# A graph network's edge sums on one core: the copies of the tiles' products out of PSUM move from ScalarE to VectorE, and ScalarE brings in a tile of rows in every ninth half chunk

## The chip, the core and the metric

The kernel runs on one core of a Trainium2 chip. The core has TensorE (PE: matrix products, with PEld for its weight loads), VectorE (DVE), ScalarE (ACT), GpSimd (POOL) and SyncE (SP), each with its own queue of instructions that it takes in order; engines wait for one another through semaphores. Transfers are started by three of these queues: SyncE and ScalarE start plain ones, GpSimd the indirect ones that gather rows by a list of numbers.

The metric is the device's time in microseconds (us) for one execution. Before the change it is 23621.08 us, the median of three runs (23593.12 to 23628.34).

## What is computed

There are 50000 nodes with 128 features each, 800000 edges between them (every pair in both directions) and one loop per node, 850000 rows of (src, dst, relation) sorted by dst. Two layers of a relational graph network run one after the other, then a residual and a layer norm:

```python
def _rgcn_layer(h, src, dst, rel, basis, w_comp, loop_w, bias):
    W = jnp.einsum('rb,bio->rio', w_comp, basis)
    seg = dst.astype(jnp.int32) * N_REL + rel.astype(jnp.int32)
    agg = jax.ops.segment_sum(h[src], seg, num_segments=N_ENT * N_REL)
    agg = agg.reshape(N_ENT, N_REL, -1)
    msg = jnp.einsum('nri,rio->no', agg, W)
    out = msg + h @ loop_w + bias
    return jax.nn.relu(out)
...
x = _layernorm(x + _L0_gnn_ref(x, ...), axis=-1)
```

All is in float32; there are 16 relations and 8 bases.

## The kernel before

The edges without the loops are cut into 6250 tiles of 128 edges. Ten tiles (K) make a chunk, five (PER) a half chunk: 625 chunks (C) and 1250 half chunks in each of the two layers. For each tile the kernel

- brings in the 128 source rows, 512 bytes each, into a buffer named g;
- multiplies them on TensorE (L1136) with a one-hot table that carries the edges' weights in each basis and their place among the chunk's nodes. The tile's product is 96 columns wide; the five products of a half chunk stand side by side in one PSUM tile, pa, of which there are three;
- copies pa into aT (L1150), where four chunks (BATCH) are gathered.

When four chunks are complete, TensorE multiplies aT with the bases (L815), the result by_slot is copied (L819), turned (L824), spread over four columns of nodes by VectorE (L798), and added to the nodes' sums (L859). Beside this run the loops' part (L745 to L780: transposes, products with the bases on TensorE, products and sums on VectorE), the weights and one-hot tables of the chunks to come (L638, L667, L950, on VectorE), and the ending of each group of 512 nodes (L881 to L894). In the first layer VectorE also sorts the edge lists as they are needed.

The rows come in by three ways. GpSimd gathers a whole tile with one indirect transfer (L186) into a ring of 30 buffers (RING x PER); it is given the gathers of the half chunk that lies 30 tiles ahead, and each waits until its buffer's product is done. The other two ways are row by row: SyncE and ScalarE bring in some tiles with 128 single transfers (L1046), and load the rows' addresses, 32 at a time, into registers (L1039). Which tiles they take is set by `takers`: the last tile of some half chunks, one in 9 for SyncE and one in 10 for ScalarE, by `SPANS = (9, 10)`. The first such half chunk is number max(SPANS) + LEAD + 6, which is 24 for SyncE. Each of the two has three buffers (HELD) for this.

The order is written out by hand (`manual_schedule`): every queue has its instructions in the order in which the loops below emit them. After each tile's product, `beside` emits one step of everything else: the rows of the tiles that SyncE and ScalarE are bringing in (`copying`; a tile's 128 rows are spread over the 45 or 50 tile steps that end 8 half chunks, LEAD, before its use), the loops' part (`owning`), the batch's sums (`summing`), the weights (`weighing`) and the ending groups. So the rows stand in ScalarE's queue between its copies, and in SyncE's between its other loads and stores.

Of the kernel before, what the change touches and what calls it, by code (L numbers as in the profile page):

```python
# [54 lines left out]
K = P // WN  # L55
# [13 lines left out]
WEIGHTS = AT * PER * 8  # L69
BITS_AT_ONCE = BANK - WEIGHTS  # L70
RING = 6
SPANS = (9, 10)
LEAD = 8
THEN = 3
HELD = 3
SEMS = 8
LOADED = 32
# [15 lines left out]
def tile_rgcn_resnorm(  # L93
# [15 lines left out]
    nc = tc.nc  # L109
    N, D = x.shape  # L110
    NR, NB = w_comp1.shape
    E = edges.shape[1] // 3
    R, M = -(-E // RUN), E - N
    C = -(-M // (K * P))
# [83 lines left out]
    def column(j, first, ap):  # L198
# [10 lines left out]
    apart = [  # L209
        [consts.tile([P, D], F32, name=f"g{RING * PER + HELD * i + j}") for j in range(HELD)] for i in range(len(APART))  # L210
    ]
    came = [[tc.alloc_semaphore(f"came{i}_{j}") for j in range(SEMS)] for i in range(len(APART))]
    uses = [0] * len(APART)
    earliest = (max(SPANS) + LEAD + 1) // 2 + 1
    far = consts.tile([P, len(ROWS), P], I32, name="far")

    def takers():

        of, first = {}, max(SPANS) + LEAD + 6
        for i, span in enumerate(SPANS):  # L220
            for q in range(first + span * i // len(SPANS), 2 * C - LEAD, span):
                while q in of:
# [388 lines left out]
    def chunked():  # L611
        with (
# [182 lines left out]
            def spread_out(c, to, of):  # L795

                k, pair = ks(c) * WN, of.shape[1]
                nc.vector.tensor_tensor(  # L798
                    to[:k],
                    of[:k, :, None, :].to_broadcast([k, pair, J, D]),  # L800
                    which[:k, c : c + pair, :, None].to_broadcast([k, pair, J, D]),
                    op=OP.mult,
                )
                return to

            def pair_of_slots():
                return sb.tile([P, 2, J, D], F32, name="slots", bufs=BATCH // 2)

            def slots_of_batch(c, aT, st, n):

                for _ in range(2):
                    yield
                ps = ps_o.tile([P, BANK], F32, name="po")
                for b in range(NB):
                    nc.tensor.matmul(  # L815
                        ps[:, : BATCH * S], BASIS[n][:, b, :], aT[:, b, :], start=b == 0, stop=b == NB - 1
                    )
                by_slot = sb.tile([P, BATCH * S], F32, name="by_slot", bufs=1)
                nc.scalar.copy(by_slot, ps[:, : BATCH * S])  # L819
                for _ in range(NB - 2):  # L820
                    yield
                po = ps_o.tile([P, BANK], F32, name="po")
                for q in range(BATCH):
                    nc.tensor.transpose(po[:S, q * P : (q + 1) * P], by_slot[:, q * S : (q + 1) * S], ident)  # L824
                    if q == 1:
                        yield
                for q in range(0, BATCH, 2):
                    pair = spread_out(c + q, pair_of_slots(), po[:, q * P : (q + 2) * P].rearrange("s (q d) -> s q d", q=2))
                    st[c + q], st[c + q + 1] = pair[:, 0], pair[:, 1]
                    yield  # L830
# [45 lines left out]
            def finish(g, n):  # L876
# [5 lines left out]
                if n == 0:  # L882
                    yield
                    nc.scalar.activation(ls, ls, AF.Relu)
                    for _ in range(THEN):
                        yield
                    nc.sync.dma_start(of_group(H1, g), ls)
                else:
                    nc.vector.scalar_tensor_tensor(ls, total, 0.0, xws.pop(g)[:m], op0=OP.max, op1=OP.add)
                    yield  # L890
                    yield from normed(ls, J, m, ls, sb)
                    for _ in range(THEN):
                        yield
# [3 lines left out]
            def done(steps):  # L897
                for _ in steps:
                    pass
# [38 lines left out]
            for n, of in enumerate((x, H1)):  # L938
# [19 lines left out]
                def sum_up(c):  # L958
                    at = c % BATCH * S
                    for st[c] in slots(c, ks(c), aTs[c // BATCH][:, :, at : at + S], n):  # L960
                        yield
# [53 lines left out]
                tiles = -(-M // P)  # L1015
# [5 lines left out]
                def row_by_row(i):  # L1021
# [3 lines left out]
                    mine = sorted(q for q in taken_by if taken_by[q] == i)  # L1025
                    for q, before in zip(mine, [mine[0] - SPANS[i], *mine]):
                        while now[1] < before - LEAD:
# [3 lines left out]
                        uses[i] += 1  # L1031
                        to, sem, group = apart[i][use % HELD], came[i][use % SEMS], f"rows{i}_{use}"
                        j = max(j for j in range(len(ROWS)) if ROWS[j] <= q)
# [46 lines left out]
                def fetch(some):  # L1080

                    for t in some:
                        if t < tiles:
                            if t % WIDE == WIDE // 2:
                                numbers(t // WIDE + 1)
                            if not alone(t):
# [4 lines left out]
                                held[t] = rows[k], came_of[k], 16 * filled_times[k], group  # L1091
                                read_now.append(group)

                numbered, held = {}, {}
                numbers(0)
                now, made = [0, 0], [0]
                owning = own_of_all()
                copying = [row_by_row(i) for i in range(len(APART))]
                for c in range(C):
                    now[0] = c  # L1100
                    if n == 0 and c:

                        next(coming, None)
                        while ready[0] + 1 < len(ROWS) and 2 * min(C, c + FETCH + earliest) > ROWS[ready[0] + 1]:
                            next(coming)
                    if c == 0:
                        fetch(range(RING * PER))
                        nc.vector.tensor_copy(table, COMP[n].rearrange("p r b -> p b r"))
                        weighing = weights(0)
                        done(weighing)  # L1110
                        hots[0] = hot_of(0)
                        hots[1] = hot_of(1)
                        if n == 0:
                            for _ in range(LBITS + 3):
                                next(first_runs)
                    if c % 2 == 0 and c + 2 < C:
                        weighing = weights(c + 2)
                    hot = hots.pop(c)
                    if c % BATCH == 0:
                        aTs[c // BATCH] = hp.tile([P, NB, BATCH * S], F32, name="aT")  # L1120
                    aT, place_of = aTs[c // BATCH], c % BATCH * S
                    if c > ALONE:
                        done(summing)
                        summing = sum_up(c - 1)
                    elif c % BATCH == 0:
                        summing = slots_of_batch(c - BATCH, aTs[c // BATCH - 1], st, n) if c else iter(())
                    for k in range(0, K, PER):
                        m = min(PER, ks(c) - k)
                        if m > 0:
                            pa = ps_a.tile([P, BANK], F32, name="pa")  # L1130
                        for i in range(PER):
                            now[1] = 2 * c + k // PER
                            if i < m:
                                t = c * K + k + i
                                row, sem, count, group = held.pop(t)
                                product = nc.tensor.matmul(  # L1136
                                    pa[:, i * NB * WN : (i + 1) * NB * WN],
                                    row,
                                    hot[:, k + i].rearrange("e b w -> e (b w)"),
                                    start=True,  # L1140
                                    stop=True,
                                ).wait_op(sem, count, "sem-ge")
                                tc.declare_fence(product.ins, group=group)
                                tc.declare_no_dep(product.ins, group=group, reason="it waits for their semaphore itself")
                            if i == m - 1:
                                at = c * K + k + RING * PER
                                fetch(range(at, at + PER))
                                if n == 0 and c == 0 and k == 0:
                                    done(first_runs)
                                nc.scalar.copy(  # L1150
                                    aT[:, :, place_of + k * WN : place_of + (k + m) * WN].rearrange(
                                        "d b (i w) -> d i b w", w=WN
                                    ),
                                    pa[:, : m * NB * WN].rearrange("d (i b w) -> d i b w", i=m, w=WN),
                                )
                            beside(k + i, c, owning, summing, weighing)
                    if c + 2 < C:
                        hots[c + 2] = hot_of(c + 2)
                    for one in added_in(c + 1) if c + 1 < C else ():
                        masks[one] = masks_of(one)  # L1160
                    if n == 0 and c == 3:
                        beginning.close()
                    if n == 0 and c == C - 1:
                        done(coming)
                        count_up(pr)
# [199 lines left out]
```

## Time and profile before

| what | value |
| --- | --- |
| device time, median of 3 runs | 23621.08 us |
| device time of the profiled execution | 23644.94 us |
| its span, first to last instruction | 23642.9 us |
| busy: PE, PEld | 11528.9 us (49%), 7370.5 us (31%) |
| busy: DVE, ACT, POOL | 10300.2 us (44%), 2154.3 us (9%), 11393.7 us (48%) |
| mean granted TensorE clock | 0.699 |
| DMA | 1014.02 MB in 585877 packets, mean 43 GB/s |

No engine is busy for half of the span, and instructions that only start a transfer are not counted as busy. In 40 equal slices of the span the engines' shares hardly change, so the kernel has one long steady stage:

```
PE   4544445445554444444555444544444444444445
DVE  5444444444444444344444444444444444444444
ACT  0000000000000000000000000000000000000001
POOL 5444444444444444444454444444444444444444
```

A digit is the busy share of a slice in tenths. A row of a group names line, engine, operation, the tile written and the tiles read, shapes and count; then busy time and the mean ns of one; then the idle time of the engine just before such instructions and what ended most of it. An engine with a q behind its name (SPq, ACTq, POOLq) is its queue starting transfers. "issue" and "remote" are idle times that the profile can put down to no other engine.

### The profile page before, as it was taken

The numbers are of one execution on the slowest core, as the hardware profiler recorded it, in microseconds if no ns is written. First come the engines' busy times: TensorE is split into PE (matmuls) and PEld (weight loads), VectorE is DVE, ScalarE is ACT, GpSimd is POOL, SyncE is SP. The second block draws the span as 40 slices with busy tenths as digits, with TensorE's granted clock in tenths as the row PEclk, the third lists the DMA queues.
The fourth block names the chain that finished last, engine by engine and source line by source line (L and its number), as shares of the span: only waits on it lengthen the run. The fifth ranks groups of instructions, "written<-read, shape, count | busy, mean of one in ns | idle before, by whom it ended". The sixth has DMA issues, their size and how long they took to land. (4 is left out here: it accounts for less than half of the span.)

```text
span 23642.9 us, 256085 instructions
## 1 busy us (share of the span) xinstructions
PE 11528.9 (49%) x43954; PEld 7370.5 (31%) x43954; DVE 10300.2 (44%) x11737; ACT 2154.3 (9%) x4309; POOL 11393.7 (48%) x12017
## 2 busy tenths in 40 slices
PE   4544445445554444444555444544444444444445
PEld 3333333333333333233333233332333233332333
DVE  5444444444444444344444444444444444444444
ACT  0000000000000000000000000000000000000001
POOL 5444444444444444444454444444444444444444
PEclk7677676766676767766766667667766677766667
DMA  2111111111111111111111111111111111111111
GB/s 58 49 46 43 45 45 47 47 42 46 48 44 41 40 39 40 40 40 40 37 48 43 42 41 41 42 42 41 41 42 42 41 42 42 41 43 41 42 42 40
DMA packets 585877, 1014.02 MB, mean 43 GB/s; under 512 B 267619, under 2 KB 336739, under 8 KB 577970
## 3 DMA queue, kind: packets, MB, share of 16 engines
q0 software_dynamic: 385360, 793.04, 12.9%
q1 hardware_dynamic: 133308, 186.60, 2.5%
q10 hardware_dynamic: 65552, 17.90, 0.3%
q14 instruction: 1302, 10.67, 0.1%
q8 instruction: 355, 5.82, 0.1%
HBM read 924.87 MB, written 71.59 MB: 42 GB/s over the span
## 5 line engine op out<-in xcount | busy, mean ns | idle before, releaser
L186 POOL DMA_INDIRECT g<-H,at x5992 | 5674.1, 947 | 6132.7 <-PE pa L1136 3704.1
L186 POOL DMA_INDIRECT g<-in_x_dram,at x5992 | 5695.0, 950 | 6012.9 <-PE pa L1136 3600.5
L1136 PE MATMUL pa<-hot,g 128*128 128x96 f32 x25000 | 4340.2, 318 | 6655.2 <-DMA g<-H 2811.6
L1136 PEld LDWEIGHTS pa<-hot,g 128*128 128x128 f32 x25000 | 4236.9, 236 | 8680.6 <-issue 3305.7
L772 DVE TENSOR_TENSOR by<-po,lw 128x512 f32<-128x512 f32 x1568 | 1076.8, 687 | 8061.4 <-PE po L765 5019.4
L859 PE MATMUL pn<-slots,own 120*128 120x512 f32 x4128 | 2763.6, 796 | 1915.6 <-issue 968.9
L765 PE MATMUL po<-basis,hT 128*128 128x512 f32 x3136 | 2134.6, 769 | 2054.3 <-issue 875.6
L815 PE MATMUL po<-aT,basis 128*128 128x480 f32 x4960 | 2451.9, 655 | 1000.3 <-ACT aT L1150 615.2
L1150 ACT COPY aT<-pa 128x480 f32<-128x480 f32 x2500 | 1394.3, 558 | 14372.9 <-issue 7359.7
L780 DVE TENSOR_REDUCE ls<-by 128x128 f32<-128x1152 f32 (+1 forms) x784 | 1656.4, 2113 | 583.9 <-DMA out_dram<-ls 427.8
L667 DVE TENSOR_REDUCE fixed<-terms 128x80 f32<-128x1280 f32 x1250 | 1864.8, 1492 | 30.4
L638 DVE TENSOR_TENSOR terms<-kinds,fixed 128x1280 f32<-128x1280 uint8 x1250 | 1849.6, 1480 | 12.1
L815 PEld LDWEIGHTS po<-aT,basis 128*128 128x128 f32 x4960 | 1079.6, 224 | 2183.3 <-issue 1544.2
L859 PEld LDWEIGHTS pn<-slots,own 120*128 120x128 f32 x4128 | 899.7, 247 | 2601.8 <-issue 1615.9
L950 DVE TENSOR_TENSOR hot<-fixed,own 128x960 f32<-128x960 f32 x1250 | 1439.3, 1152 | 313.4 <-PE pa L1136 255.7
L765 PEld LDWEIGHTS po<-basis,hT 128*128 128x128 f32 x3136 | 597.2, 237 | 2112.6 <-issue 943.2
L798 DVE TENSOR_TENSOR slots<-po,which 120x1024 f32<-120x1024 f32 (+1 forms) x630 | 761.6, 1209 | 971.2 <-remote 511.2
L881 DVE TENSOR_TENSOR pn<-pn,ls 128x512 f32<-128x512 f32 x98 | 68.1, 695 | 930.9 <-PE pn L859 394.8
L1073 ACT CAST at<-src 128x20 int32<-128x20 uint16 x626 | 129.5, 207 | 3701.2 <-issue 3688.1
L838 DVE TENSOR_SCALAR own<-col,node 120x256 f32<-120x256 f32 (+1 forms) x1250 | 426.0, 341 | 9.8 <-PE pn L859 8.6
L881 DVE TENSOR_TENSOR ls<-pn,ls 128x512 f32<-128x512 f32 x98 | 67.2, 685 | 752.3 <-PE pn L859 328.4
L703 DVE TENSOR_TENSOR both_kinds<-col,po 128x256 uint8<-128x256 f32 (+1 forms) x50 | 20.8, 416 | 841.8 <-PE po L695 476.2
(143 smaller groups left out, 4155.4 us busy)
## 6 DMA issues: line engine op xcount, KB each, us to landing
g<-in_x_dram SPq DMA_DIRECT2D x17408, 0.5 KB
g<-H SPq DMA_DIRECT2D x17408, 0.5 KB
g<-in_x_dram ACTq DMA_DIRECT2D x15616, 0.5 KB
g<-H ACTq DMA_DIRECT2D x15616, 0.5 KB
g<-in_x_dram,at POOLq DMA_INDIRECT x5992
g<-H,at POOLq DMA_INDIRECT x5992
H<-ls SPq DMA_DIRECT2D x97, 256.0 KB
xw<-in_x_dram SPq DMA_DIRECT2D x97, 256.0 KB
```

The source lines that it names most:

```text
L186: return nc.gpsimd.indirect_dma_start(out=to, out_offset=None, in_=of, in_offset=bass.IndirectOffsetOnAxis(ap=idx, axis=0))
L638: nc.vector.tensor_tensor(terms, kinds[:, :, None, :].to_broadcast([P, k, NB, NR]), table[:, None, :, :].to_broadcast([P, k, NB, NR]), op= ...
L667: nc.vector.tensor_reduce(to[:, : ks(i)], terms, AX.X, OP.add)
L765: nc.tensor.matmul(hb[:m], hT[:, j, :m], BASIS[n][:, b : b + few, :].rearrange("p b d -> p (b d)"), start=True, stop=True,)
L772: nc.vector.tensor_tensor(by[:m, b : b + few, :], hb[:m].rearrange("p (b d) -> p b d", d=D), lw[:m, j, g % T, b : b + few, None].to_broadc ...
L780: nc.vector.tensor_reduce(ls[:m, j, :], by[:m].rearrange("p b d -> p d b"), AX.X, OP.add)
L798: nc.vector.tensor_tensor(to[:k], of[:k, :, None, :].to_broadcast([k, pair, J, D]), which[:k, c : c + pair, :, None].to_broadcast([k, pair ...
L815: nc.tensor.matmul(ps[:, : BATCH * S], BASIS[n][:, b, :], aT[:, b, :], start=b == 0, stop=b == NB - 1)
L859: nc.tensor.matmul(sums[g], own, of[:k].rearrange("s j d -> s (j d)"), start=c == first(g), stop=c == final(g),)
L950: nc.vector.tensor_tensor(hot[:, : ks(c)], pm[:, : ks(c), :, None].to_broadcast([P, ks(c), NB, WN]), own[:, : ks(c), None, :].to_broadcast ...
L1136: product = nc.tensor.matmul(pa[:, i * NB * WN : (i + 1) * NB * WN], row, hot[:, k + i].rearrange("e b w -> e (b w)"), start=True, stop=Tr ...
L1150: nc.scalar.copy(aT[:, :, place_of + k * WN : place_of + (k + m) * WN].rearrange("d b (i w) -> d i b w", w=WN), pa[:, : m * NB * WN].rearr ...
```

## The change

The copy of a half chunk's products from pa to aT is no longer emitted right behind the half chunk's last product. It is kept (`to_take`) and emitted behind the first product of the next half chunk, one tile later. VectorE makes it in chunks 8 to 616; before and after these ScalarE still does. The by_slot copy stays on ScalarE and is emitted one step of the batch's sums later, and one step fewer lies between it and the transposes that read it. `SPANS` becomes (9, 9): ScalarE brings in a tile in every ninth half chunk. With it the first half chunk with such a tile becomes 23.

```diff
-SPANS = (9, 10)
+SPANS = (9, 9)
 LEAD = 8
 THEN = 3
+COPIED = 8
...
+                yield
                 by_slot = sb.tile([P, BATCH * S], F32, name="by_slot", bufs=1)
                 nc.scalar.copy(by_slot, ps[:, : BATCH * S])
-                for _ in range(NB - 2):
+                for _ in range(NB - 3):
                     yield
...
+                to_take = []
+
+                def taken_out():
+
+                    by_vector = COPIED <= now[0] < C - COPIED
+                    (nc.vector.tensor_copy if by_vector else nc.scalar.copy)(*to_take)
...
+                            if i == 0 and c + k:
+                                taken_out()
                             if i == m - 1:
                                 at = c * K + k + RING * PER
                                 fetch(range(at, at + PER))
                                 if n == 0 and c == 0 and k == 0:
                                     done(first_runs)
-                                nc.scalar.copy(
+                                to_take[:] = [
                                     aT[:, :, place_of + k * WN : place_of + (k + m) * WN].rearrange(
                                         "d b (i w) -> d i b w", w=WN
                                     ),
                                     pa[:, : m * NB * WN].rearrange("d (i b w) -> d i b w", i=m, w=WN),
-                                )
+                                ]
+                                if c * K + k + m == tiles:
+                                    taken_out()
```

In the whole program ScalarE's single rows go from 31232 to 34560 (26 tiles more), SyncE's stay 34816, and GpSimd's gathers fall by 26. The first place to look at is ScalarE's queue around the by_slot copy of one batch in the second layer. Before:

```order
L1150 COPY aT<-pa 128x5x8x12
L1046 DMA g_122<-H_57 1x512 x2
L1039 TENSOR_LOAD far
L1046 DMA g_120<-H_57 1x512 x5
L819 COPY by_slot<-po 128x480
L1046 DMA g_120<-H_57 1x512 x5
L1150 COPY aT<-pa 128x5x8x12
L1046 DMA g_120<-H_57 1x512 x2
L751 COPY hT<-po 128x4x128
```

And now, around the same copy (lines have moved by one or two):

```order
L1075 CAST at<-src 128x20
L1048 DMA g_122<-H_57 1x512 x17
L752 COPY hT<-po 128x4x128
L821 COPY by_slot<-po 128x480
L1048 DMA g_122<-H_57 1x512 x8
L602 ACTIVATE sd<-mv,eps 128x4
L1048 DMA g_122<-H_57 1x512 x2
L1041 TENSOR_LOAD far
L1048 DMA g_122<-H_57 1x512 x18
```

The aT copies between the rows are gone, so ScalarE's queue has only the hT and by_slot copies and the ending of a group between rows that wait for other engines, and by_slot now stands behind hT.

The second place is VectorE's queue in the second layer, where a group of nodes ends and a batch is spread into slots. Before:

```order
L638 TENSOR_TENSOR terms<-kinds,fixed 128x1280
L667 TENSOR_REDUCE fixed<-terms 128x80
L881 TENSOR_TENSOR pn<-pn,ls 128x512
L889 SCALAR_TENSOR_TENSOR ls<-pn,xw 128x512
L950 TENSOR_TENSOR hot<-fixed,own 128x960
L838 TENSOR_SCALAR own<-col_128,node_126 120x128
L598 BN_STATS st<-ls 128x6
```

Now:

```order
L1101 COPY aT<-pa 128x5x8x12
L639 TENSOR_TENSOR terms<-kinds,fixed 128x1280
L668 TENSOR_REDUCE fixed<-terms 128x80
L883 TENSOR_TENSOR pn<-pn,ls 128x512
L891 SCALAR_TENSOR_TENSOR ls<-pn,xw 128x512
L952 TENSOR_TENSOR hot<-fixed,own 128x960
L840 TENSOR_SCALAR own<-col_128,node_126 120x128
L1101 COPY aT<-pa 128x5x8x12
L599 BN_STATS st<-ls 128x6
```

The rest of VectorE's queue keeps its order; a copy stands in it twice in each chunk, ahead of the weights of a chunk to come and behind its one-hot table and its masks.

## The prediction, made before the changed kernel had run

> **What bounds the kernel now.** The reading starts with the view of who waited for whom, to see whether any compute engine is short. These are its rows on TensorE's products, on GpSimd's gathers and on ScalarE's copies: total us, times, longest.
>
> ```profile
> POOL g L186 <- PE pa L1136: 7304.7, 784, 37.3
> ...
> ACT aT L1150 <- PE pa L1136: 5011.9, 682, 35.2
> ...
> PE pa L1136 <- DMA g<-H: 2811.6, 123, 38.5
> ...
> PE pa L1136 <- DMA g<-in_x_dram: 2398.1, 105, 39.5
> ...
> PE pa L1136 <- ACT aT L1150: 683.6, 118, 38.1
> ...
> PE po L815 <- ACT aT L1150: 615.2, 83, 14.8
> ```
>
> GpSimd waits 7304.7 us for a free row buffer, so it is not short. TensorE waits 2811.6 + 2398.1 = 5209.7 us for gathered rows, but in only 228 waits of about 23 us. That is close to the number of tiles that SyncE brings in row by row, and far from the number of GpSimd's gathers. So the second look is the view of tile g, which has every transfer of rows: count, shortest/median/longest ns, first and last start.
>
> ```profile
> L1136 PE MATMUL pa<-hot,g x25000: 242/275/529, 41.5 to 23626.6; 128*128 128x96 f32 x199
> ...
> L1046 SPq DMA_DIRECT2D g<-in_x_dram x17408: 1/228/1486, 104.4 to 11758.0; - x198
> ...
> L1046 SPq DMA_DIRECT2D g<-H x17408: 1/228/1532, 11830.8 to 23562.6; - x198
> ...
> L1046 ACTq DMA_DIRECT2D g<-in_x_dram x15616: 2/235/1407, 166.5 to 11688.8; - x198
> ...
> L1046 ACTq DMA_DIRECT2D g<-H x15616: 2/235/1462, 11939.6 to 23494.0; - x198
> L186 POOL DMA_INDIRECT g<-in_x_dram,at x5992: 939/947/1816, 30.3 to 11801.7; - x200
> L186 POOL DMA_INDIRECT g<-H,at x5992: 939/947/1122, 11830.1 to 23609.1; - x200
> ```
>
> SyncE issues 17408 rows in each layer, 128 to a tile: 136 tiles, one in every 9 half chunks. Its two streams last 11653.6 and 11731.8 us. Together that is 23385.4 of the span's 23642.9 us; only 257.5 us lie before, between and after them. Does the stream ever rest? The view of SyncE's own waits has as its longest row:
>
> ```profile
> SPq L887 <- ACT ls L884: 62.4, 3, 42.2
> ```
>
> So it hardly waits. And TensorE starts again when a tile of it is complete, as the transfers issued up to 6062.5 us (first fence) and TensorE's row of the timeline (second) show:
>
> ```profile
> g<-in_x_dram SPq DMA_DIRECT2D x8832, 0.5 KB
> ```
>
> ```profile
> 6063.74 0.53 PE L1136 MATMUL pa<-hot,g 128*128 128x96 f32 x1 [20.80 <-DMA g<-in_x_dram]
> ```
>
> 8832 is 69 times 128: the 69th tile's last row had been issued by 6062.5 us, and TensorE's wait of 20.80 us ended at 6063.74. **SyncE's issuing of rows is the bound.** Everything else has 5209.7 / 272 = 19.2 us of cover for each SyncE tile.
>
> **What sets SyncE's pace.** A median row takes 228 ns to issue, yet the mean is 23385.4 / 34816 = 0.672 us. Five windows of 15 us, by engine (busy us and instructions of PE, PEld, DVE, ACT, POOL; then TensorE's clock, DMA share, GB/s), tell why:
>
> ```profile
> 14907.00:14922.00 15.00, 0.00 (x0) 0.00 (x0) 0.00 (x0) 0.00 (x0) 0.00 (x0) 0.50 0.03 11
> 2458.00:2473.00 15.00, 8.12 (x15) 4.19 (x16) 14.47 (x17) 2.25 (x5) 0.00 (x0) 0.56 0.06 21
> 11831.00:11846.00 15.00, 6.88 (x22) 5.22 (x22) 12.40 (x10) 0.56 (x1) 11.34 (x13) 0.50 0.26 76
> 11849.00:11864.00 15.00, 9.55 (x30) 7.43 (x30) 0.00 (x0) 0.56 (x1) 11.34 (x13) 0.50 0.20 53
> 12976.00:12991.00 15.00, 10.16 (x36) 5.49 (x36) 10.04 (x9) 0.56 (x1) 10.64 (x12) 1.00 0.21 54
> ```
>
> The transfers issued in the same five windows, one fence for each:
>
> ```profile
> g<-H SPq DMA_DIRECT2D x39, 0.5 KB
> ```
>
> ```profile
> g<-in_x_dram SPq DMA_DIRECT2D x40, 0.5 KB
> g<-in_x_dram ACTq DMA_DIRECT2D x38, 0.5 KB
> ```
>
> ```profile
> g<-H SPq DMA_DIRECT2D x24, 0.5 KB
> g<-H,at POOLq DMA_INDIRECT x13
> ```
>
> ```profile
> g<-H,at POOLq DMA_INDIRECT x13
> g<-H SPq DMA_DIRECT2D x7, 0.5 KB
> ```
>
> ```profile
> g<-H,at POOLq DMA_INDIRECT x12
> g<-H ACTq DMA_DIRECT2D x12, 0.5 KB
> g<-H SPq DMA_DIRECT2D x8, 0.5 KB
> ```
>
> Without gathers SyncE issues 39 or 40 rows in 15 us, 0.385 us each with its loads of offsets, and 38 rows of ScalarE beside them, or a VectorE that is busy for 14.47 us, take nothing from it. With gathers back to back it issues 24 rows while the run is young, and 7 or 8 later, the same with ScalarE silent (7) as with 12 of its rows (8). So a gather costs SyncE (15 - 24 x 0.385) / 13 = 0.44 us early in a run and (15 - 7 x 0.385) / 13 = 0.95 us late. On the mean: 23385.4 - 34816 x 0.385 = 9981 us over 11984 gathers, 0.83 us each.
>
> The Trainium skill reads such a stall otherwise: its page "DMA: Bandwidth & Descriptors", in the section "Issuing engines are not separate DMA queues", says that transfers from all issuing engines end on the same 16 DMA engines and interleave, and that several issuers save only the sequencers' time. By that a tile moved from GpSimd to ScalarE would relieve SyncE of nothing, and the first term below would be 0, the sum +12.6 us. The windows speak against it: SyncE falls from 39 rows to 7 while the DMA engines are busy to a share of only 0.20.
>
> **The change part by part.** The sum is made against the profiled execution, 23644.94 us by the device's time, 0.10% above the median of the three runs, 23621.08.
>
> *ScalarE's tiles in every 9th half chunk.* Its spacing falls from 10 to 9, so it brings 135 tiles a layer in place of 122, 26 more in all, and GpSimd gathers 26 fewer. For SyncE this is worth between nothing and a gather's whole slot in a back-to-back run, 15 / 12 = 1.25 us (last window); I take the mean of 0.83: **-21.6 us**. The 26 tiles are 3328 more rows on ScalarE's queue. Their price to SyncE lies between 0 and, if the two queues excluded each other, 0.235 us a row, 782 us. The two pairs of windows (40 against 39, 8 against 7) stand at 0: **0 us**.
>
> *SyncE's tiles one half chunk earlier.* They stand at 23 + 9k instead of 24 + 9k, again 136 a layer. The stream starts where it did, and one more half chunk follows its end. In the second layer the last SyncE row is issued at 23562.6 and the last product starts at 23626.6: 10 half chunks in 64 us, 6.3 us each (from 0, if the tail is shortened elsewhere, to 9.5, the span over 2500 half chunks). Twice that: **+12.6 us**.
>
> *The copies.* 2436 of 2500 copies go from ScalarE to VectorE. Two rows of groups, with mean ns after the busy time:
>
> ```profile
> L772 DVE TENSOR_TENSOR by<-po,lw 128x512 f32<-128x512 f32 x1552 | 1066.1, 687 | 8001.7 <-PE po L765 4962.2 <-remote 1216.5 <-issue 1186.2
> ...
> L1150 ACT COPY aT<-pa 128x480 f32<-128x480 f32 x2500 | 1394.3, 558 | 14372.9 <-issue 7359.7 <-PE pa L1136 5011.9 <-remote 1541.1
> ```
>
> VectorE reads 512 elements from PSUM in 687 ns, so a copy of 480 should take 480/512 of it, 0.64 us (an estimate, between ScalarE's 0.558 and the 0.687 itself): 1559 us, or 5.7 us per SyncE tile. Queued behind the waiting copy are VectorE's weights, one-hot tables and loop products, for which TensorE waits. Even if all 5.7 us land on TensorE's path, and none of the 683.6 + 615.2 us (4.8 per tile) in which TensorE waited for ScalarE's copies comes back, the cover of 19.2 us holds: **0 us**. Without that cover it would be +1559 us.
>
> *The by_slot copy one step later.* It stays on ScalarE, its readers stand where they stood: **0 us**, under the same cover.
>
> Sum: -21.6 + 12.6 = **-9 us**. Against the median that is 23612 us: no change. A measurement of this kernel tells about 0.2%, 47 us, from no change.
>
> **The rivals.** *A: ScalarE becomes the bound (slower).* In the second layer its rows took (23494.0 - 11939.6) / 15616 = 0.740 us, 94.7 us a tile; SyncE's period, which it now has to keep, is 23385.4 / 272 = 86.0. It must win back 8.7 us a tile. It can: before its copies ScalarE's datapath sat idle for 5011.9 us until a product was done, and 1541.1 us with no releaser told, up to 26.9 us for each of its 244 tiles, though rows were issued in part of that. The rival decides if less than 8.7 us come back. Each us that is missing costs 272 us; with 3 missing the time is 24.43 ms, with nothing won 25.98 ms. Against it: TensorE's waits for rows, 228, are fewer than SyncE's tiles alone, and a ScalarE that lags no longer waits. Chance 0.10.
>
> *B: gathers run in longer runs (slightly slower).* TensorE, no longer held at ScalarE's copies, frees row buffers more evenly, and GpSimd's 784 waits become fewer. A gather moved from early to late in a run costs 0.95 - 0.44 = 0.51 us, and one such per SyncE tile 272 x 0.51 = 139 us. B decides from a third of a gather per tile; with one, 23751 us. Chance 0.14.
>
> *C: the runs get shorter (faster).* The same price with the other sign: VectorE, in order and fuller, holds TensorE at more places, GpSimd pauses more often, and ScalarE, free of its waits, uses the pauses for its rows. One gather per tile from late to early gives 23473 us, one and a half 23404. For it: 5.7 us of new VectorE work per tile against 4.8 us of waits that go. Chance 0.27. The skill's page "SBUF — State Buffer", section "Who interferes with whom", would add to C: a VectorE copy in a two-port mode locks GpSimd out for its whole length. But "VectorE: DVE Perf Modes", section "Why PSUM operands drop a tier", takes a source in PSUM out of that mode, so I add nothing for it; no row here shows such a copy.
>
> *D: ScalarE's rows do cost SyncE.* At up to 0.235 us for each of 3328 rows: 24.39 ms. The windows with ScalarE's rows speak against it. Chance 0.05.
>
> **How the numbers follow.** The forecast, within 0.2% either way (23565 to 23659), has 0.44. Faster is C, 0.27; slower are A, B and D, 0.29. The range takes in B and C to one and a half gathers per tile, 23612 less or plus 209: 23400 to 23830; outside are A, D and the ends of B and C, about 0.2. The predicted time is the forecast's, 23612.
>
> **What would show it.** Right: SyncE's two streams again fill all but some 270 us of the span; GpSimd has 11958 gathers; TensorE still waits some 5000 us for gathered rows, in about 230 long waits; its waits for ScalarE's aT copies are gone. A: waits for rows that end when ScalarE's tiles are complete, and more than 272 of them. B or C: the number of GpSimd's waits for TensorE's products clearly under or over 784, and SyncE's mean row off 0.672 us. D: SyncE's rows slower in windows without gathers. The forecast is wrong above all if SyncE's streams no longer fill the span.

## The result, and the profile after

On the chip of the prediction the changed kernel takes 23524.13 us, the median of six runs (23493.53 to 23546.47); the kernel before takes 23608.2 us (six runs, three of them those of before the prediction). The ratio is 0.9965, with an interval of 0.9954 to 0.9975: 84 us faster. The time lies in the predicted range, 88 us under the forecast of 23612. It is no "no change" by the bound of 0.2% that the prediction set itself: it falls on rival C's side, and it is the width that the range gave to C, not the sum of -9 us, that takes it in.

That is half of the result. The experiments below ran on chips 12, 7 and 15, and there **the kernel before takes 15118.9 to 15139.3 us, and the same changed kernel is 4.2% slower** (timed on chip 7). The first measurements name no chip. That theirs was another one is taken from the times alone; it is called the first chip here. So there are two questions: where 84 us went on the first chip, and why the sign turns on the others.

First the page of the changed kernel on the first chip: its span, its busy times and the chain that ended last, which could be followed back through a part of the span only.

```profile
span 23544.3 us, 262043 instructions
...
PE 11586.5 (49%) x43954; PEld 7419.2 (32%) x43954; DVE 11688.0 (50%) x14173; ACT 838.5 (4%) x1873; POOL 11364.1 (48%) x11991
...
SPq 12%; issue 7%; PE 1%; ACTq 0%; DVE 0%; DMA 0%; ACT 0%; another core or an unknown queue 0%; DVEq 0%
```

The copies have moved: ScalarE is busy for 838.5 us in place of 2154.3, VectorE for 11688.0 in place of 10300.2. Then the view of tile g, with the transfers of rows: count, shortest/median/longest ns, first and last start.

```profile
L1048 SPq DMA_DIRECT2D g<-in_x_dram x17408: 1/228/1477, 103.9 to 11666.0; - x198
...
L1048 SPq DMA_DIRECT2D g<-H x17408: 1/228/1450, 11745.0 to 23461.1; - x198
...
L1048 ACTq DMA_DIRECT2D g<-in_x_dram x17280: 2/228/1450, 145.3 to 11532.5; - x199
...
L1048 ACTq DMA_DIRECT2D g<-H x17280: 2/228/1412, 11852.9 to 23346.5; - x199
L187 POOL DMA_INDIRECT g<-in_x_dram,at x5979: 939/947/1819, 30.2 to 11714.9; - x200
L187 POOL DMA_INDIRECT g<-H,at x5979: 939/947/1083, 11744.4 to 23510.7; - x200
```

SyncE's streams last 11562.1 us (11653.6 before) and 11716.1 us (11731.8 before). Together they lose 107.2 us; the stretch between them grows by 6.2 us, the tail by 2.9 us, and the start loses 0.5 us: 98.6 us between the two profiled spans. Most of the gain, 91.5 us, is in the first layer. And who waited for whom, in the rows that answer to those shown before:

```profile
POOL g L187 <- PE pa L1145: 7059.8, 728, 48.6
...
PE pa L1145 <- DMA g<-H: 2934.2, 121, 41.5
...
PE pa L1145 <- DMA g<-in_x_dram: 2288.7, 94, 38.6
...
PE po L766 <- ACT hT L752: 924.0, 66, 29.4
...
PE po L816 <- DVE aT L1101: 752.6, 87, 46.4
...
PE pa L1145 <- DVE aT L1101: 97.8, 10, 39.0
```

TensorE's waits for rows are 5222.9 us in 215, against 5209.7 us in 228. Its waits for copies have moved: the tiles' products wait for aT for 97.8 us in place of 683.6, while the products with the bases wait 752.6 us in place of 615.2 for aT and 924.0 in place of 858.9 for hT. The bound is still SyncE's rows.

### The profile page after: what moved, and what is told of

The parts are those of the page before. It is cut to its first block, busy times and chain, and to the rows that moved or that the text cites. A ratio compares the mean times of both kernels' runs of the same rounds, so it can differ in the third digit from the quotient of the medians.

```text
span 23544.3 us, 262043 instructions
## 1 busy us (share of the span) xinstructions
PE 11586.5 (49%) x43954; PEld 7419.2 (32%) x43954; DVE 11688.0 (50%) x14173; ACT 838.5 (4%) x1873; POOL 11364.1 (48%) x11991
## 5 line engine op out<-in xcount | busy, mean ns | idle before, releaser
L1145 PE MATMUL pa<-hot,g 128*128 128x96 f32 x25000 | 4289.6, 317 | 5679.3 <-DMA g<-H 2934.2
L816 PE MATMUL po<-aT,basis 128*128 128x480 f32 x4960 | 2572.1, 681 | 1366.1 <-DVE aT L1101 752.6
L766 PE MATMUL po<-basis,hT 128*128 128x512 f32 x3136 | 2118.3, 764 | 1753.8 <-ACT hT L752 924.0
L1101 DVE COPY aT<-pa 128x480 f32<-128x480 f32 x2436 | 1567.6, 648 | 2672.5 <-PE pa L1145 2143.6
L826 PE MATMUL po<-ident,by_slot 128*120 128x128 f32 x1240 | 311.5, 343 | 743.5 <-DVE by L773 423.0
L826 PEld LDWEIGHTS po<-ident,by_slot 128*120 128x120 f32 x1240 | 190.9, 188 | 764.1 <-issue 634.0
L746 PE MATMUL po<-ident,h_own 32*128 32x32 f32 x3136 | 328.2, 249 | 60.1 <-issue 54.1
```

The costliest lines, as they stand in the source:

```text
L766: nc.tensor.matmul(hb[:m], hT[:, j, :m], BASIS[n][:, b : b + few, :].rearrange("p b d -> p (b d)"), start=True, stop=True,)
L816: nc.tensor.matmul(ps[:, : BATCH * S], BASIS[n][:, b, :], aT[:, b, :], start=b == 0, stop=b == NB - 1)
L1101: (nc.vector.tensor_copy if by_vector else nc.scalar.copy)(*to_take)
L1145: product = nc.tensor.matmul(pa[:, i * NB * WN : (i + 1) * NB * WN], row, hot[:, k + i].rearrange("e b w -> e (b w)"), start=True, stop=Tr ...
```

## The experiments

All times below are against the kernel before on the same chip. "The copies alone" and "SPANS alone" undo one half of the change each; the third keeps the new order but leaves the copies on ScalarE; the fourth gives SyncE, not ScalarE, the wider spacing. In the second the diff is against the kernel before, in the others against the changed kernel.

```diff
e1_copies_only
-SPANS = (9, 9)
+SPANS = (9, 10)
e2_spans_only
-SPANS = (9, 10)
+SPANS = (9, 9)
e3_late_on_scalar
-SPANS = (9, 9)
+SPANS = (9, 10)
-COPIED = 8
+COPIED = 400
e4_sync_every_10th
-SPANS = (9, 9)
+SPANS = (10, 9)
```

> The changed kernel with ScalarE's tiles back in every 10th half chunk; the copies on VectorE, the later place and the later by_slot copy stay. GpSimd has 11984 gathers again and SyncE its old places. If the gain of 84 us came from 26 fewer gathers and their 0.83 us alone, the time is that of before, about 23600 us. If it came from the copies (gathers in shorter runs, ScalarE's queue without waits for products), about 85 - 9 us of it is here: some 23530 us, and SyncE's first stream stays some 80 us shorter than before.

> The kernel before with only the spacing changed to (9, 9); the copies stay on ScalarE. By the forecast's terms (26 gathers fewer, a longer tail) -9 us: about 23600 us. If ScalarE cannot bring in a tile in 86 us while its queue waits at copies (rival A), each us that it is short costs 272 us: 23.8 ms and more, with waits of TensorE that end when ScalarE's tiles are complete.

> Spacing (9, 10) and all copies on ScalarE, but emitted one tile later, and the by_slot copy one step later, as in the changed kernel. If the later places matter, some of the 84 us are here; if VectorE's taking the copies matters, the time is that of before, 23600 us within 30.

> The changed kernel with SyncE's tiles in every 10th half chunk, ScalarE's in every 9th: 122 SyncE tiles a layer instead of 136, some 28 more gathers. If SyncE's issuing is the bound at 0.385 us a row and 0.83 to 0.95 us a gather, a period of 10 half chunks takes 89 to 91 us: 22.05 to 22.45 ms, 5 to 6% faster. If its stream only fills the span because its rows are spread over it and something else sets the pace, the time stays at 23.5 ms.

Measured on chip 12, where the kernel before takes 15138.93 us:

| run | time, us | ratio | interval |
| --- | --- | --- | --- |
| e1, copies alone | 15197.70 | 1.0039 | 1.0025 to 1.0053 |
| e2, SPANS alone | 15757.12 | 1.0407 | 1.0393 to 1.0421 |
| e3, late, on ScalarE | 15141.86 | 1.0002 | 0.9992 to 1.0011 |
| e4, SyncE every 10th | 15306.25 | 1.0110 | 1.0092 to 1.0128 |

None of the expectations was made for a chip of 15.14 ms, so the numbers in them miss. What bounds the kernel here is seen in e3, which takes as long as the kernel before. The groups of its page (busy, mean ns, idle before) and the waits' row:

```profile
L187 POOL DMA_INDIRECT g<-in_x_dram,at x5992 | 5695.6, 951 | 1845.5 <-issue 1701.3
L187 POOL DMA_INDIRECT g<-H,at x5992 | 5671.8, 947 | 1849.7 <-issue 1720.5
```

```profile
POOL g L187 <- issue: 3421.9, 11138, 19.6
```

A gather takes 0.95 us as on the first chip, and GpSimd hardly waits for anybody: it goes from one gather to the next after a pause of 3421.9 / 11138 = 0.31 us that no engine ends. 5695.6 + 5671.8 + 3421.9 = 14789 of the span's 15140.0 us are this. **GpSimd is the bound here**, and SyncE keeps up with it. Why it can is in one row of e3's tile g against the same row of the changed kernel on the first chip, the MOVE that stands before each row's transfer:

```profile
L1048 SPq MOVE g<-in_x_dram x17408: 29/29/38, 86.5 to 7498.4; - x198
```

```profile
L1048 SPq MOVE g<-in_x_dram x17408: 1/29/1409, 103.9 to 11666.0; - x198
```

An instruction of 29 ns that moves no data takes up to 1409 ns in this row on the first chip and never over 38 here. No stall such as the prediction put at 0.83 us a gather is seen here.

But e2, with 26 gathers fewer, is 4% slower. Two theories: the fuller row queue of ScalarE is the bound (A'), or the place of the copies behind rows (Q). The changed kernel itself belongs beside e2, and spacings on both sides of it. The diffs are against the changed kernel; e5 has none.

```diff
e6_scalar_every_18th
-SPANS = (9, 9)
+SPANS = (9, 18)
e7_both_every_12th
-SPANS = (9, 9)
+SPANS = (12, 12)
e8_both_every_8th
-SPANS = (9, 9)
+SPANS = (8, 8)
```

> The changed kernel as it is, beside the kernel before on the chip of these runs. Where the kernel before takes about 23.6 ms (SyncE's issuing of rows is the bound): 0.9965 of it again, about 23525 us. Where it takes about 15.14 ms (GpSimd is the bound, a gather's slot is 15 / 12 = 1.25 us or 0.947 us and the pause behind it): theory G, that only the gathers and the copies' place count, gives the time with the copies alone moved, 15197.7 us, less 26 x 1.25 = 32 us, 15165 us, ratio 1.002. Rival Q, that ScalarE's fuller row queue holds TensorE whoever makes the copies (its hT and by_slot copies stand behind rows too), gives the 15757 us of the run in which only SPANS was changed, or a good part of it: over 15300 us.

> The changed kernel with SPANS = (9, 18): ScalarE brings in 67 tiles a layer in place of 135 (and SyncE 135 in place of 136), so GpSimd gathers 138 more in all. Where SyncE's issuing is the bound: 138 x 0.83 = +115 us from the changed kernel, about 23.62 ms, and over 23.9 ms slower is excluded; if ScalarE's rows did cost SyncE (rival D, up to 0.235 us each of 17408 fewer), up to 4 ms faster. Where GpSimd is the bound: 138 x 1.25 = +172 us from the changed kernel, about 15.34 ms; if ScalarE's queue holds TensorE (rival Q), the same or faster than the changed kernel.

> The changed kernel with SPANS = (12, 12): 102 + 101 tiles a layer row by row in place of 136 + 135, GpSimd gathers 136 more in all (12094). Where SyncE's issuing is the bound, its two streams become 26112 x 0.385 + 12094 x (0.83 to 0.95) = 20.1 to 21.5 ms and the time 20.3 to 21.8 ms, over 7% faster; if the streams are only the place where TensorE waits, and something that doesn't scale with SyncE's rows is the bound, 23.5 to 23.7 ms. Where GpSimd is the bound: 136 x 1.25 = +170 us, about 15.34 ms.

> The changed kernel with SPANS = (8, 8): 153 + 152 tiles a layer row by row, GpSimd gathers 68 fewer in all (11890). Where SyncE's issuing is the bound, its streams become 39168 x 0.385 + 11890 x 0.83 = 24.95 ms and the time 25.2 ms, 7% slower. Where GpSimd is the bound: 68 x 1.25 = -85 us from the changed kernel, about 15.08 ms, faster than both kernels, unless ScalarE's or SyncE's rows become the bound there: at 0.24 to 0.40 us a row (31 to 51 us a tile, a period of 48) that is near.

Measured on chip 7, where the kernel before takes 15118.89 us:

| run | time, us | ratio | interval |
| --- | --- | --- | --- |
| e5, the change as it is | 15757.20 | 1.0421 | 1.0407 to 1.0436 |
| e6, ScalarE every 18th | 15236.97 | 1.0079 | 1.0063 to 1.0094 |
| e7, both every 12th | 15236.36 | 1.0077 | 1.0059 to 1.0096 |
| e8, both every 8th | 17299.39 | 1.1442 | 1.1421 to 1.1463 |

The change takes 15757.20 us, e2 15757.12: who makes the copies is worth nothing once SPANS is (9, 9). That compares two chips whose kernels before differ by 20 us; e11 below makes the same comparison on chip 12. Theory G, 15165 us, is wrong by 592 us, and the number of theory Q came out. Fewer rows on ScalarE (e6) bring the time down by 520 us although GpSimd has 138 gathers more, and e8 goes up to 17.3 ms, where its expectation had 15.08 ms for a kernel bound by GpSimd and called ScalarE's rows near to being the bound. The expectations of e6 and e7, 15.34 ms, are 100 us too high. e6 has 112 gathers more than the kernel before and takes 118 us more, 1.05 us for each, less than the 1.25 us of a gather's slot, and nothing is left for the copies on VectorE.

The changed kernel on chip 7 shows how a late ScalarE looks. Rows of tile g and of the waits:

```profile
L1048 ACTq DMA_DIRECT2D g<-in_x_dram x17280: 227/228/928, 120.5 to 7767.8; - x199
...
L1048 ACTq DMA_DIRECT2D g<-H x17280: 227/228/717, 7977.6 to 15602.4; - x199
```

```profile
POOL g L187 <- issue: 3417.4, 11131, 18.1
...
PE po L766 <- ACT hT L752: 1461.4, 167, 20.4
...
POOL g L187 <- PE pa L1145: 858.4, 600, 11.8
...
PE pa L1145 <- DMA g<-H,at: 112.1, 165, 2.5
```

ScalarE's streams last 7647.3 + 7624.8 = 15272 us for 270 tiles, 56.6 us each. At the pace of a kernel that is bound by GpSimd (15140 us for 2500 half chunks) nine half chunks last 54.5 us. ScalarE takes 2.1 us more than it would be given. By itself that is only the spacing of the slower kernel; but e8, with a spacing of eight, takes 17299.39 x 8 / 2500 = 55.4 us for a tile where GpSimd's pace would give 48.4, so the time of a tile hardly follows the spacing. And yet TensorE does not wait for rows that came one by one (the view has no such row): its longest wait is for hT, 1461.4 us against 158.9 in e3. The last row of a tile is written into the queue 8 half chunks ahead of the tile's use, but the hT copy stands in the same queue, behind rows that are late, and is needed soon. TensorE's waits for VectorE's masks (1040.6 us against e3's 178.9) and slots (698.1 against 159.2) are longer too. GpSimd then waits for buffers that TensorE holds, 858.4 us in place of e3's 170.4:

```profile
POOL g L187 <- PE pa L1145: 170.4, 558, 0.3
...
PE po L766 <- ACT hT L752: 158.9, 75, 6.4
```

Is it the issuing of rows itself, or hT's place? Three kernels ask. In two of them one transfer writes its row into two partitions, so one engine issues half as many; every second row of these tiles then holds its neighbour's data, and the two are run for their times alone. The third takes the hT and by_slot copies off ScalarE.

```diff
e9_scalar_two_rows
+                    two = 2 if i == 1 else 1
...
-                                    to[e : e + 1, :].bitcast(U8),
-                                    flat[ds(places[e % LOADED], 4 * D)].rearrange("(o d) -> o d", o=1),
+                                    to[e : e + two, :].bitcast(U8),
+                                    flat[ds(places[e % LOADED], 4 * D)].rearrange("(o d) -> o d", o=1).broadcast_to((two, 4 * D)),
...
-                                e += 1
+                                e += two
-                        held[q * PER + PER - 1] = to, sem, 16 * P * (use // SEMS + 1), group
+                        held[q * PER + PER - 1] = to, sem, 16 * (P // two) * (use // SEMS + 1), group
e10_sync_two_rows (the rest as in e9)
+                    two = 2 if i == 0 else 1
e11_all_copies_on_vector
-                nc.scalar.copy(
+                nc.vector.tensor_copy(
                     hT.rearrange("d j (p a) -> d a j p", a=A)[:, :, :, :rows_in],
...
-                nc.scalar.copy(by_slot, ps[:, : BATCH * S])
+                nc.vector.tensor_copy(by_slot, ps[:, : BATCH * S])
```

> The changed kernel, but each of ScalarE's row transfers writes its source row into two partitions, so a tile of ScalarE takes 64 transfers in place of 128 (every second row of these tiles holds its neighbour's data; bytes, loads of addresses and gathers stay). On a chip where the kernel before takes about 15.1 ms: theory A', that ScalarE's queue cannot issue a tile's 128 rows and its copies within nine half chunks of GpSimd's pace (15757 x 9 / 2500 = 56.7 us needed, 15140 x 9 / 2500 = 54.5 us there), gives back what SPANS cost: 15.12 to 15.20 ms. Rival: the rows' bytes or the copies' place in the order hold the kernel, not the issuing: 15.7 ms stays. Where the kernel before takes 23.6 ms: within 1% of the changed kernel if ScalarE's rows cost SyncE nothing; up to 17280 x 0.235 us = 4 ms less if they do (rival D).

> The same done to SyncE's row transfers instead of ScalarE's. Where the kernel before takes about 15.1 ms: by theory A' SyncE is not what is late, so the time stays near the changed kernel's 15757 us, unless SyncE's rows slow ScalarE's down: with SyncE at every tenth half chunk ScalarE's tile took 15306 x 9 / 2500 = 55.1 us in place of 56.7, and by that half of the rows would give 15.12 to 15.3 ms. If SyncE's own issuing were the bound there, also 15.1 to 15.2 ms, and then the run of ScalarE's two rows would change nothing. Where the kernel before takes 23.6 ms and SyncE's issuing is the bound: 17408 transfers fewer, at least 17408 x 0.26 = 4.5 ms off the streams until ScalarE's rows (94.7 us a tile there) become the bound: 20 to 23 ms, at least 2% faster than the changed kernel.

> The changed kernel with the copies of hT and by_slot on VectorE too, so that no product of TensorE has to wait for a copy in ScalarE's queue. Where the kernel before takes about 15.1 ms: by theory A' ScalarE is still the bound but has 381 us of copies less, 1.4 us a tile and what they waited: a tile of 54.5 to 55.3 us, 15.15 to 15.4 ms, and TensorE's waits move from hT to ScalarE's rows or go. Rival: only the hT copies' place behind the rows costs time, the rows themselves have room: under 15.17 ms and no waits for rows of ScalarE. Where the kernel before takes 23.6 ms: within 1% of the changed kernel.

Measured on chip 12 again, where the kernel before takes 15139.32 us:

| run | time, us | ratio | interval |
| --- | --- | --- | --- |
| e9, ScalarE two rows | 15103.82 | 0.9977 | 0.9967 to 0.9986 |
| e10, SyncE two rows | 15248.39 | 1.0071 | 1.0054 to 1.0088 |
| e11, all copies on VectorE | 15759.79 | 1.0409 | 1.0392 to 1.0427 |

e9 settles it: the same gathers, bytes, loads of addresses and copies, but half of ScalarE's transfers, and the whole loss is gone, with 35 us on top, 16 us more than expected. That is about what 26 gathers are worth (26 x 1.25 = 33 us). Its chain ends with GpSimd; that of e11 with ScalarE's queue. First e9's:

```profile
POOL 23%; PE 11%; issue 8%; DVE 4%; DMA 4%; ACTq 0%; ACT 0%; POOLq 0%; DVEq 0%
```

Then e11's:

```profile
ACTq 27%; issue 5%; DVE 4%; PE 3%; ACT 0%; DVEq 0%
```

e11 missed its expectation of 15.15 to 15.4 ms, and so did theory Q: nothing of TensorE's needs ScalarE's copies any more in most of the kernel, and the time stays (e2, with all copies on ScalarE, took 15757.12 us on the same chip). The waits have moved. One of them is GpSimd's, for the copy that makes its row numbers and still stands behind rows on ScalarE:

```profile
POOL g L187 <- ACT at L1075: 209.2, 126, 8.5
```

That the 1.4 us of copies a tile bring nothing has its reason in the timeline of ScalarE. In the changed kernel on chip 7 (start, us, engine, line, operation; the idle time is that of the arithmetic part alone):

```profile
12014.88 1.20 ACTq L1048 DMA_DIRECT2D g<-H  x4
12016.12 1.06 ACT L752 COPY hT<-po 128x512 f32<-128x512 f32 x1 [7.78 <-issue]
12016.20 14.71 ACTq L1048 DMA_DIRECT2D g<-H  x37
```

The copy starts at 12016.12 and runs for 1.06 us; the next row's transfer is issued at 12016.20, 0.08 us later. Over the 506 copies of hT and by_slot in that trace the median from a copy's start to the next row is 75 ns; some are followed by a load of addresses or a wait. A copy whose operands are ready costs the queue 0.08 us, not its length. And 37 rows take 14.71 us, 0.40 each: with a median transfer of 228 ns it is the instructions around it and the loads of addresses that make up the rest.

e10 shows a price that the prediction had not looked for: it asked what ScalarE's rows cost SyncE (rival D), not the other way round. SyncE's transfers slow ScalarE's: with half of them the time is 15248.39 x 9 / 2500 = 54.9 us per ScalarE tile in place of 56.7, at least 1.8 us for 64 transfers fewer, some 28 ns each (a bound, since other waits end the path there too). Over all records of a trace the mean length of ScalarE's row transfers is 260 ns in e2 and 268 in e11, and 239 in e10, on the same chip. It is no fixed price for a transfer: in e4 SyncE has only a tenth fewer, 12.8 for each of ScalarE's tiles, and the tile takes 1.6 us less, 0.13 us for each; the mean length there is 243 ns. The other direction is in the traces as well: SyncE's row transfers last 251 ns on the mean in e2, 258 in e11 and 232 in e9, beside half of ScalarE's. So the 56.7 us are what ScalarE needs beside all of SyncE's rows, and fewer transfers of either queue help.

The last run asks whether A' also predicts a spacing: with both at 10, ScalarE has room again.

```diff
e12_both_every_10th
-SPANS = (9, 9)
+SPANS = (10, 10)
```

> The changed kernel with SPANS = (10, 10): 122 + 122 tiles a layer row by row, 12012 gathers, 28 more than before and 54 more than in the changed kernel. Where the kernel before takes about 15.1 ms: if ScalarE's queue was what SPANS (9, 9) and (10, 9) ran into, GpSimd is the bound again and only its gathers count: the kernel with the copies alone moved (1.0039) and 28 x 1.25 = 35 us, ratio 1.006, which is faster than (10, 9) with 1.0110 although 26 gathers more are made; if not, slower than (10, 9) by those 26 gathers, ratio 1.013. Where the kernel before takes 23.6 ms: SyncE's streams shrink to 31232 x 0.385 + 12012 x (0.83 to 0.95) = 22.0 to 23.4 ms and the time to 22.25 to 23.7 ms, faster than the changed kernel if SyncE's issuing is the bound there; 23.5 to 23.6 ms if it isn't.

Measured on chip 15: 15188.36 us against 15124.27 us before, ratio 1.0043 (1.0029 to 1.0057). It makes 26 gathers more than e4 (on chip 12) and its ratio is lower by 0.7%, as A' has it. In e4, ScalarE's tile in every 9 half chunks took 15306.25 x 9 / 2500 = 55.1 us, more than the 54.5; here it has ten half chunks, 60.8 us.

No version that computes the whole was faster than the kernel before on these chips; e3 equals it. On the first chip the changed kernel is the fastest that was run. The wider spacings, which by the expectations would help there most, couldn't be tried there: none of the experiments ran on that chip.

## Why the prediction was right, and where it was not

**The bound.** SyncE's issuing, on the first chip: right. Its streams fill all but 266 us of the changed span (some 270 forecast), and the 215 long waits for rows stayed.

**26 gathers fewer, -21.6 us, and the mean price of 0.83 us.** The count came out (11958). The price was held constant, and here the sum failed: (11562.1 + 11716.1 - 34816 x 0.385) / 11958 = 0.826 us in place of 0.833. The streams lost 107.2 us; 21.7 of them are the 26 gathers, and 85.5 are 0.007 us on each of the others. This term of the sum, 0 for a change of the price, was mis-sized; rival C had named it. Its sign was left to chance, and the marker that the prediction gave for it fails: GpSimd's waits went down from 784 to 728, which it had read as longer runs, B.

Did the runs get shorter, as C has it? Counted from the starts of GpSimd's indirect transfers (a run: less than 1.4 us apart), SyncE issues 2.5 to 2.7 rows beside a gather at the first two places of a run, 1.2 at the sixth and some 0.6 from the eighth on, in both kernels. So a gather is late from the eighth place on. Of these the first layer has 1741, against 1807 before, and the second 1876, against 1809: 66 fewer and 67 more, nothing over both layers. (From the thirteenth place on it is 299 against 387 and 336 against 337; the answer hangs on where late is taken to begin.) **The time moved the way that C forecast, but shorter runs are not shown.** What made the price lower stays open, and whether the copies or the spacing did it wasn't tried on that chip. The price is also a remainder, not a cost measured at the gathers: outside the runs SyncE's rows take 0.47 us each on the mean, before and after, and not the 0.385 of the two windows.

**The tail, +12.6 us.** Between the streams and behind the last one 9.1 us came: the size is about right. (64 us over ten half chunks are 6.4 us each, not 6.3.)

**The copies, 0 us under a cover of 19.2 us a tile.** The mean is 648 ns, against 0.64 us forecast:

```profile
L1101 DVE COPY aT<-pa 128x480 f32<-128x480 f32 x2436 | 1567.6, 648 | 2672.5 <-PE pa L1145 2143.6 <-remote 460.9 <-PE po L746 32.6
```

Some of what the prediction allowed not to come back did: the tiles' products wait 97.8 us for aT in place of 683.6. The products with the bases wait 752.6 us in place of 615.2; TensorE still waited 215 times for rows, so the cover was not used up. Where GpSimd is the bound the copies cost 59 us with SPANS (9, 10) (e1); in the same order on ScalarE they cost 3 us, within the interval (e3), so it is not the tile of delay. But they cost nothing beside fewer transfers (e6, e9), and of e12's 64 us some 30 are left when its 28 gathers are paid, so it is no fixed price. The near explanation is that TensorE waits longer for VectorE's slots and masks behind the copies. It can make up a part at most. e1's rows:

```profile
PE pn L861 <- DVE slots L799: 444.2, 149, 9.9
PE pn L861 <- DVE own L840: 432.0, 236, 4.2
```

And e9's, which are only 95 us shorter in sum, without a loss (e3 has 159.2 and 178.9 us):

```profile
PE pn L861 <- DVE slots L799: 405.1, 124, 9.9
PE pn L861 <- DVE own L840: 375.7, 208, 4.7
```

What the 59 us are stays open.

**Rival A.** Its chance of 0.10 stood on a misread row. ScalarE's 94.7 us a tile before was no need of ScalarE: ten half chunks at 23642.9 / 2500 = 9.46 us are 94.6 us, so the row only showed when rows were asked for. After the change a tile takes (11532.5 - 145.3) / 135 = 84.3 and (23346.5 - 11852.9) / 135 = 85.1 us, again its spacing, 9 x 9.42 = 84.8. There was nothing to win back; A didn't come on the first chip, but not for the reasons that the prediction gave against it. On the others it did, with its mechanism as written (ScalarE's rows too many for the spacing) and another way of showing itself: waits for hT, not for rows.

**Rival D.** That ScalarE's rows cost SyncE wasn't seen on the first chip and wasn't tried there. That rows of the two queues slow each other is shown elsewhere: SyncE's transfers are 232 ns beside half of ScalarE's rows (e9) and 251 to 258 beside all, 19 to 26 ns, and not the 235 ns for each row of rival D.

**Why the sign turns.** On the first chip half chunks come every 9.42 us and ScalarE has 84.8 us for a tile. On the others they come every 6.06 us; it has 54.5 and needs 56.6 beside all of SyncE's rows. The prediction rests on SyncE's stall beside gathers, which the same kernel shows in the first measurements and not in the later ones. One window of the changed kernel on chip 7 answers to the prediction's last windows: first the busy times, then the transfers issued.

```profile
12060.00:12075.00 15.00, 11.36 (x52) 8.32 (x51) 13.76 (x16) 0.00 (x0) 11.16 (x12) 0.83 0.35 73
```

```profile
g<-H ACTq DMA_DIRECT2D x33, 0.5 KB
g<-H SPq DMA_DIRECT2D x32, 0.5 KB
...
g<-H,at POOLq DMA_INDIRECT x12
```

Twelve gathers back to back, and SyncE issues 32 rows beside 33 of ScalarE; on the first chip it was 8 beside 12.

**Left open.** What makes the first chip stall; whether it is the chip, or something else in which the first measurements differ from the later ones; and which half of the change gave the 84 us there.

## What to carry to other kernels

How long a paced queue takes for its work is its spacing, not its need: before a queue is given more, halve its transfers once and see whether the time follows. Beside a need that lies within a few per cent of the spacing, a small step of the spacing (10 to 9) costs many times what it saves. A wait for a small copy can be the sign of a full issuing queue ahead of it: here moving the copy away moved the wait, and only fewer transfers ended it. And a balance found on one chip should be timed on a second.

## What the runs showed of the hardware

- The same kernel takes 23608.2 us in the first measurements and 15118.9 to 15139.3 us on chips 12, 7 and 15. The instructions that were compared last as long on both (a gather 947 ns, the copy of 480 columns 648 and 647 ns); what differs is that SyncE's and ScalarE's issuing stalls beside gathers in the first, down to a MOVE of 29 ns that takes up to 1409. The granted TensorE clock differs too: 0.699 there and 0.807 on chip 12.
- Row transfers of one issuing engine make those of another longer, with SPANS (9, 9): 260 to 268 ns on ScalarE beside all of SyncE's, 239 beside half of them; 251 to 258 ns on SyncE beside all of ScalarE's, 232 beside half. The Trainium skill's page "Perfetto Trace Analysis", in the section "DMA Instruction — HWDGE (DVE, Sync)", has a block that writes the descriptors, is shared by two issuing engines and is locked for one instruction at a time, and says that the profile counts the wait for the lock into the instruction. The page's heading names VectorE and SyncE, and adds that which two engines issue is the compiler's choice. e10 agrees with it in kind; no run here shows the lock itself.
- ScalarE issues transfers while it copies: 0.08 us after the start of a copy that lasts 1.06 us the next row was issued, and 75 ns is the median over 506 copies of the trace of e5.
